# Recurrence and expert layer on one core: when the third group's token rows leave, and the places of slot products, a maximum, a unit's turn and weight pieces

## The chip, the cores and the metric

The kernel runs on one core of a Trainium2 chip. Its metric is the device time in microseconds of one execution. The time before the change is 388.15 us, the median of 6 runs that lie between 387.39 and 389.12 us. A core has a matrix engine (TensorE, called PE in the profile, with PEld for the loading of its weights), VectorE (DVE), ScalarE (ACT), GpSimd (POOL) and SyncE (SP), which issues most of the DMA transfers. Each engine works through its own instructions in order; engines wait for each other by semaphores.

## What is computed

A tanh recurrence over 1024 steps for two sequences, and on its states a layer of eight experts of which each token uses two; the result is added to the input.

```python
xW = jnp.einsum('ntd,dh->nth', x, Wx) + b
def step(prev_h, xw_t):
    next_h = jnp.tanh(xw_t + prev_h @ Wh)
    return (next_h, next_h)
_, hs = jax.lax.scan(step, h0, jnp.swapaxes(xW, 0, 1))
...
logits = x_flat @ gate_w.T
top_v, top_i = jax.lax.top_k(logits, K)
probs = jax.nn.softmax(top_v.astype(jnp.float32), axis=-1).astype(logits.dtype)
combine = jnp.einsum('tk,tke->et', probs, one_hot)
def body(acc, ws):
    wge, wue, wde, we = ws
    hidden = jax.nn.silu(x_flat @ wge.T) * (x_flat @ wue.T)
    return (acc + we[:, None] * (hidden @ wde.T), None)
...
x = x + _L0_ffn_ref(_L0_cond_ref(x, cond_1024, Wx, Wh, b), gate_w, wg, wu, wd)
```

There are 2048 tokens of 256 numbers, 8 experts (E), 1024 hidden numbers per expert (I) and K = 2.

## The kernel before

**The recurrence.** The 1024 steps are cut into 64 chunks of 16 steps per sequence, and all chunks run side by side; each starts early, from a state that isn't exact, and a check at the end compares the starts of the chunks with the ends of the chunks before (`chunk_starts` at L538, `starts_check` at L673). The loop over `s` from 8 to 63 (L612) is one chain: four products of the state with `Wh` (two halves `j` of the output, two halves `k` of the state; eight PE records in float32, L619), two tanh on ScalarE, and `seed` (L307), which puts the input part of step `s + 2` into the accumulators: half 0 on VectorE, half 1 on ScalarE. The last 16 steps, 48 to 63, give the token tiles 0 to 15, each of 128 tokens.

**The route.** While the chain runs, tiles are routed in four groups of four. `route_tile` (L348) is a PE product that turns a tile into rows of 264 numbers, 256 of the state and 8 logits. `route_max` finds the two best experts on VectorE. `route_choice`, `route_position` (PE, L395) and `route_code` give each token its place in the list of its expert; `route_onehot` builds three large one-hot arrays of 128 x 1024 (parts 0, 1 and 2) on VectorE, and `route_slots` (L438) multiplies them on PE into the table `inv_ps`, which says for each slot of each expert which token stands there. `rows_out` (L377) sends a group's rows to `rows_d` in memory by SyncE: two transfers of 256 KB for the states and later one of 16 KB for the weights that replace the logits.

**The gathers.** `early_slots` (L471) runs once groups 0 and 1 are in the table: it computes the index `gidx` for the first 256 slots of expert 0, and two indirect DMAs of GpSimd gather these rows from the first half of `rows_d`. `early_turn` (L480) turns them on PE into the layout that the experts need, and unit 0 starts. `all_slots` (L483) does the same for the rest once group 3 is in: `gidx`, a copy `inv`, two more gathers (the late tiles, for unit 1), and what the order of the experts needs.

**The experts.** A unit is up to 512 slots of one expert. Unit 0 and unit 1 are the two halves of expert 0, unit 2 is expert 1, and the other six experts follow in the order of their counts, worked out by `expert_order` (L492), a generator of five pieces of work that are called one at a time. A unit has eight steps of 128 hidden numbers. One step has a `front` (12 PE products, L717), a `gate` (silu on ScalarE, product on VectorE, then a split of the result into a high half by a ScalarE cast and a low half by VectorE), and a `back` (L879) two steps later. `units[i].turn()` turns the gathered rows of a unit on PE and splits them on ScalarE and VectorE. The next expert's weights are split into high and low halves in six pieces (`Job.piece`, L762: ScalarE 128 x 1024 for the high half, VectorE for the low half); `split_at` says in which step each stands, and an odd piece, once done, issues the load for the expert after it on SyncE.

**The order.** Most instructions stand in the order in which Python issues them (`vec`, `act`, `pool` and `pe(...)` fix it). Around the chain and the first steps of the experts, the order is written as due times: `at(t, f)` files a piece of work and `run(t)` issues all that is due, by time. In step `s` of the recurrence, `run(s - 0.5)` stands after the second of the four products and `run(s)` at the end. In step `n` of the experts, `run` is called with 64 + n + 0.15 after the front, + 0.2 ahead of `shut(n)` (the gate), + 0.3 after it, and + 0.6 after the backs. These calls fix the order on every engine:

```python
if i == 2:
    run(s - 0.5)
...
u.front(s)
run(64 + n + 0.15)
...
run(64 + n + 0.2)
if n > 0:
    shut(n)
```

Unit 0's steps are n = 0 to 7, unit 1's 8 to 15, and unit 2 starts at n = 16. At n = 3 the back of step 0 is issued, at n = 4 those of steps 1 and 2, and from n = 5 on that of step n - 2.

Of the kernel before, what the change touches and what calls it, by code (L numbers as in the profile page):

```python
# [8 lines left out]
F32 = mybir.dt.float32  # L9
# [10 lines left out]
P = 128  # L20
# [4 lines left out]
E = 8  # L25
# [32 lines left out]
def rnn_moe(ctx, tc, xT, xrows, h0T, Wx, Wh, b, gw, W, out):  # L58
    nc = tc.nc
    pe = tc.keep_in_program_order  # L60
# [3 lines left out]
    dram = ctx.enter_context(tc.tile_pool(name="dram", bufs=1, space=DRAM))  # L64
    ov = ctx.enter_context(tc.tile_pool(name="ov", bufs=1))
    wctx = ctx.enter_context(ExitStack())

    rows_d = dram.tile([NT, ROW], F32, name="rows_d")


    ig = cst.tile([P, 2, P + E], F32, name="ig")
# [71 lines left out]
    def ptr_tile():  # L143
        return pl.ptp.tile([P, 512], F32, name="ptr", tag="ptr")
# [53 lines left out]
    def token_parts(pool, n):  # L198
        return [pool.tile([P, 2, n * P], F32R, name=f"{nm}{n}") for nm in ("xhi", "xlo")]
# [120 lines left out]
    early_tiles, late_tiles = [], []  # L320
# [19 lines left out]
    for g in range(R // GRP):  # L340
        o = (g % 2) * 4 * GRP * P
        gr = {"r0": g * GRP, "n": GRP}
# [34 lines left out]
    def rows_out(gr, cs):  # L377
        a, b = gr["r0"] * P, (gr["r0"] + gr["n"]) * P
        for o, e in cs:
            nc.sync.dma_start(rows_d[a:b, o:e].rearrange("(i p) c -> p i c", p=P), gr["rows"][:, :, o:e])  # L380

    def route_exp(gr):
        gr["ex"] = rt.tile([P, gr["n"]], F32, name="ex")
# [73 lines left out]
    def gather(idx, rows=rows_d):  # L457
        xg = pl.gp.tile([P, ROW], F32, name="xg")
        nc.gpsimd.indirect_dma_start(  # L459
            out=xg, out_offset=None, in_=rows[:, :],  # L460
            in_offset=bass.IndirectOffsetOnAxis(ap=idx, axis=0),
        )
        return xg
# [7 lines left out]
    def early_slots():  # L471
# [3 lines left out]
        scatter_index(sidx[:, 0:ET], inv_e, eq_e)  # L475
        early_tiles.extend(gather(gidx[:, i : i + 1], rows_d[0 : NA * P, :]) for i in range(ET))

    x4 = token_parts(pl.xp, MT)

    def early_turn():  # L480
# [63 lines left out]
    def at(step, f, *args):  # L544
        todo.setdefault(step, []).append(lambda: f(*args))

    def run(step):
        for t in sorted(t for t in todo if t <= step):
            for f in todo.pop(t):
                f()  # L550
# [8 lines left out]


    maxima = {r: r + 49.5 for r in range(R)}
    maxima.update({9: 59.5, 10: 60.6, 11: 61, 12: 62.2, 13: 62.3, 14: 64.05, 15: 64.06})
    for g, gr in enumerate(groups):
        for r in range(gr["r0"], gr["r0"] + gr["n"]):
            at(r + 49, route_tile, gr, r)
# [2 lines left out]
    def group(g, choice, exp, position, code, hot, slots):  # L568
        gr = groups[g]
        at(choice, route_choice, gr)  # L570
        at(exp, route_exp, gr)
        at(choice + 0.1, rows_out, gr, ((0, P), (P + E, ROW)))
        at(position, route_position, gr)
        at(code, route_code, gr)
        at(code, rows_out, gr, ((P, P + E),))
        for part, t in enumerate(hot):
            at(t, route_onehot, gr, part)
        for i in range(gr["n"]):
            at(slots, route_slots, gr, i)

    group(0, 52.5, 52.6, 53.5, 53.5, (54, 54, 55), 56.5)
    group(1, 56.5, 56.6, 57.5, 57.5, (58, 58, 58), 59.9)
    at(58.1, early_gap)
    at(60, early_slots)
    group(2, 61, 61.1, 62, 62, (62.4, 64.1, 64.1), 65.12)
    at(63.5, early_turn)
    group(3, 64.07, 64.08, 65.1, 65.13, (65.2, 65.3, 66.3), 67.65)
    at(64.09, act.activation, warm, zl[:, 0:1], AF.Silu)
    at(67.65, all_slots)
    at(68.6, chunk_starts)  # L590

    inj = {}
    for s, q in ((15, 2), (31, 1), (47, 0)):
# [18 lines left out]
    for s in range(S0, 64):  # L612
# [7 lines left out]
        n, late = (s - S0 + 3) // 2, None  # L620
# [35 lines left out]
        n = (s - S0 + 6) // 2  # L656
# [9 lines left out]
    def starts_flag(ps):  # L666

        pe(nc.tensor.matmul(ps, lhsT=ones16, rhs=okh, start=True, stop=True))
        vec.tensor_scalar(flags[:, 0:1], ps, P - 0.5, None, ALU.is_lt)
        vec.tensor_tensor(flags[:, 2:3], flags[:, 0:1], flags[:, 1:2], ALU.add)  # L670
        vec.tensor_copy(flags_i, flags)

    def starts_check():  # L673
        vec.tensor_tensor(df, df, df, ALU.mult)
        vec.tensor_scalar(df, df, TOL * TOL, None, ALU.is_le)
        vec.tensor_reduce(okm, df, AX.XYZ, ALU.min)
        vec.tensor_copy(okh, okm)
# [30 lines left out]
    with ExitStack() as c2:  # L708
# [187 lines left out]
        units = [Unit(jobs[0], cols=ET * P, tiles=early_tiles), Unit(jobs[0], t0=ET, cols=(MT - ET) * P, tiles=late_tiles)]  # L896
# [17 lines left out]
        split_at = {}  # L914
        for j in range(len(jobs) - 1):
            two = sum(u.job is jobs[j] for u in units) > 1
            for n, m in enumerate((2, 3, 4, 6, 7) if not two else (5, 7, 10, 11, 12, 15) if j == 0 else (3, 4, 7, 10, 12, 15)):
                split_at[j, m] = j + 1, n
            if not two:
                split_at[j + 1, 0] = j + 1, 5  # L920
        order_ops = expert_order()

        def shut(n):

            u, s, j, m = step_of(n)
            low = []
            if (j, m) in split_at:
                to, p = split_at.pop((j, m))
                u.gate(s, lambda: low.append(jobs[to].piece(p, jobs[to + 1] if to + 1 < len(jobs) else None)))
            else:  # L930
                u.gate(s)
            for f in low:
                f()
# [8 lines left out]
        for n in range(len(steps)):  # L942
            i, s = steps[n]
            u = units[i]
            u.front(s)

            run(64 + n + 0.15)
            if n == 1:
                shut(0)
# [3 lines that stand above are left out]
            run(64 + n + 0.3)  # L953
            if n == 16:
                starts_check()
            elif n == 20:
                next(order_ops, None)
                starts_flag(ptr_tile()[:, 0:1])

            if s == (6 if i == 0 else 5) and i + 1 < len(units):  # L960
                if i == 0:
                    units[1].gather()
                    units[2].gather()
                units[i + 1].turn()
            for _ in range({4: 1, 6: 1, 8: 2, 9: 1}.get(n, 0)):
                next(order_ops)
            if i > 0 and s == 2 and i + 2 < len(units):
                units[i + 2].gather()
            if n < len(steps) - NIC + TAIL + 2:

                for late in {2: (), 3: (0,), 4: (1, 2)}.get(n, (n - 2,) if n > 4 else ()):
                    v, t = steps[late]
                    units[v].back(t)
            run(64 + n + 0.6)
        assert not split_at

# [181 lines left out]
```

## Time and profile before

| what | value |
|---|---|
| median of 6 runs | 388.15 us (387.39 to 389.12) |
| time of the profiled execution | 387.87 us |
| its span, first to last instruction | 385.9 us |
| mean granted TensorE clock | 0.994 |
| PE waits at route_slots (L442) | 1.7 us in 2 waits |
| PE waits for the early gathers (L208) | 1.6 us in 2 waits |
| early gathers, POOL start | 71.30 and 72.79 us |
| first front of unit 0 | 78.84 us |
| late gathers, POOL start | 90.81 and 92.10 us |
| first front of unit 1, of unit 2 | 98.34, 116.26 us |
| row stores of a 256 KB kind, median to landing | 2.7 us (groups 0, 1, 3), 4.0 us (group 2) |
| gathers through `gidx`, median to landing | 2.9 us |

Times in the timeline count from the start of the span. A line of it gives the start, the duration, the engine, the source line, the operation with what it writes and reads, and in brackets how long the engine had been idle before it and who released it. L54 is the line of a helper through which all instructions of VectorE, ScalarE and some of GpSimd are issued, so there one goes by the names of the tiles: `wd<-iota,m` is a one-hot array (built in the space of a weight tile), `xg<-rows_d,gidx` a gather, `pgu_t<-hl` a seed, `g<-g,pgu_t` the product of a gate. PE's instructions overlap, so the next one starts before the one before is shown to end.

### The profile page before, as it was taken

Reading aid. Unit: us, or ns where it says so; the run is one execution under the profiler, and the core shown is the slowest. Engines: PE = TensorE matmul, PEld = TensorE weight load, DVE = VectorE, ACT = ScalarE, POOL = GpSimd, SP = SyncE. Lnnn points to the kernel's source line nnn. Section 1 sums busy time; section 2 is a strip of 40 time slices with the busy share of each in tenths; the row PEclk is TensorE's granted clock in tenths of the full one; section 3 lists DMA queues with packets and bytes.
Section 4 is the critical chain, followed back from the end, with each engine's and each line's share of the span. In section 5 each row is a group of like instructions: output and inputs, shape, how many; then the busy total and the mean of one; then the engine's idle time right before and its main releaser. Section 6 shows DMA issues by size and latency. Waiting matters only on the chain.

```text
span 385.9 us, 7242 instructions
## 1 busy us (share of the span) xinstructions
PE 369.5 (96%) x2715; PEld 349.4 (91%) x2715; DVE 227.0 (59%) x568; ACT 199.0 (52%) x460; POOL 116.9 (30%) x124
## 2 busy tenths in 40 slices
PE   8999999898999999999999999999999999999990
PEld 8998899788998889999999999999989999999890
DVE  6876648767776566565547554566545645663410
ACT  3746667544565544655446544665354555444420
POOL 3780000304282510783223601522050014006042
PEclk9999999999999999999999999999999999999997
DMA  7962334321465333665145243345133244003122
GB/s 222 404 259 100 109 111 114 87 56 45 140 177 182 60 113 129 151 206 132 48 122 139 57 124 116 59 137 138 44 94 115 59 160 54 0 2 40 12 23 35
DMA packets 19225, 42.20 MB, mean 109 GB/s; under 512 B 4800, under 2 KB 14176, under 8 KB 16064
## 3 DMA queue, kind: packets, MB, share of 16 engines
q1 hardware_dynamic: 12400, 32.32, 24.7%
q0 software_dynamic: 6496, 9.09, 14.6%
q8 instruction: 23, 0.38, 0.4%
q10 hardware_dynamic: 288, 0.26, 0.3%
q14 instruction: 18, 0.15, 0.1%
HBM read 35.15 MB, written 9.14 MB: 115 GB/s over the span
## 4 chain that ended last, share of the span: by engine, by line
PE 86%; DVE 3%; POOL 3%; issue 2%; DMA 2%; ACT 2%; POOLq 0%
PE pgu_t L717 47%; PE yb L879 22%; PE pgu_t L619 9%; PE ptr L301 2%; DMA xg<-rows_d,gidx 2%; PE ptr L208 2%; POOL out_dram L466 2%; DVE wd L54 1%; PE ptr L630 1%; PE ptr L355 1%; ACT h L54 1%; PE pgu_t L879 1%; PE ptr L879 1%; POOL xg L459 1%; DVE hh L54 0%
## 5 line engine op out<-in xcount | busy, mean ns | idle before, releaser
L879 PE MATMUL yb<-wd,hh 128*128 128x256 f32 (+2 forms) x544 | 94.1, 283 | 0.0
L54 DVE TENSOR_TENSOR g<-g,pgu_t 128x256 f32<-128x256 f32 (+5 forms) x96 | 50.1, 522 | 60.0 <-PE pgu_t L717 47.4
L879 PEld LDWEIGHTS yb<-wd,hh 128*128 128x128 f32 (+2 forms) x544 | 80.5, 185 | 1.7
L54 ACT CAST hh<-g 128x256 fp32r<-128x256 f32 (+5 forms) x92 | 44.6, 485 | 69.5 <-DVE g L54 68.7
L466 POOL DMA_INDIRECT out_dram<-y,si x27 | 43.8, 1621 | 118.5 <-ACT y L54 113.0
L717 PE MATMUL pgu_t<-xhi,gu_g 128*128 128x256 f32 (+5 forms) x384 | 78.1, 325 | 0.3 <-ACT xhi L54 0.3
L717 PE MATMUL pgu_t<-xhi,gu_u 128*128 128x256 f32 (+5 forms) x384 | 77.8, 324 | 0.0
L54 ACT ACTIVATE g<-pgu_t 128x256 f32<-128x256 f32 (+5 forms) x96 | 44.8, 467 | 63.8 <-PE pgu_t L717 63.1
L717 PEld LDWEIGHTS pgu_t<-xhi,gu_u 128*128 128x128 f32 x384 | 61.3, 188 | 4.3
L717 PEld LDWEIGHTS pgu_t<-xhi,gu_g 128*128 128x128 f32 x384 | 58.8, 189 | 2.8 <-issue 0.5
L54 DVE TENSOR_TENSOR hl<-g,hh 128x480 fp32r<-128x480 f32 (+4 forms) x52 | 31.0, 597 | 31.8 <-ACT hh L54 31.8
L879 PE MATMUL yb<-wd,hl 128*128 128x256 f32 (+1 forms) x176 | 49.6, 282 | 0.0
L717 PE MATMUL pgu_t<-xlo,gu_g 128*128 128x256 f32 (+5 forms) x192 | 46.6, 324 | 0.0
L717 PE MATMUL pgu_t<-xlo,gu_u 128*128 128x256 f32 (+5 forms) x192 | 46.5, 323 | 0.0
L459 POOL DMA_INDIRECT xg<-rows_d,gi x27 | 29.4, 1090 | 48.9 <-DVE cm L808 19.7
L717 PEld LDWEIGHTS pgu_t<-xlo,gu_g 128*128 128x128 f32 x192 | 32.5, 188 | 2.3
L717 PEld LDWEIGHTS pgu_t<-xlo,gu_u 128*128 128x128 f32 x192 | 32.5, 188 | 2.2
L879 PEld LDWEIGHTS yb<-wd,hl 128*128 128x128 f32 (+1 forms) x176 | 32.2, 183 | 0.1
L54 DVE TENSOR_TENSOR hh<-g,hh 128x256 fp32r<-128x256 f32 x40 | 17.0, 425 | 22.4 <-ACT hh L54 22.4
L619 PE MATMUL pgu_t<-h,wh 128*128 128x128 f32 (+1 forms) x224 | 28.6, 266 | 1.5
L54 ACT ACTIVATE h<-pgu_t 128x128 f32<-128x128 f32 (+1 forms) x72 | 17.6, 276 | 13.8 <-PE pgu_t L619 11.5
L619 PEld LDWEIGHTS pgu_t<-h,wh 128*128 128x128 f32 x152 | 18.4, 190 | 4.3 <-ACT h L54 3.4
(166 smaller groups left out, 462.4 us busy)
## 6 DMA issues: line engine op xcount, KB each, us to landing
raw<-in_W_dram SPq DMA_DIRECT2D x24, 1024.0 KB, 5.0
gu_u<-in_xT_dram SPq DMA_DIRECT2D x6, 256.0 KB, 4.8
rows_d<-gu_u SPq DMA_DIRECT2D x6, 256.0 KB, 2.7
out_dram<-in_xrows_dram SPq DMA_DIRECT2D x1, 512.0 KB, 15.0
rows_d<-rows SPq DMA_DIRECT2D x2, 256.0 KB, 4.0
xg<-rows_d,gi POOLq DMA_INDIRECT x27, 3.2
out_dram<-y,si POOLq DMA_INDIRECT x27, 3.9
gu_u<-in_xT_dram ACTq DMA_DIRECT2D x2, 128.0 KB, 3.6
```

What stands on the lines that cost most here:

```text
L54: return lambda *a, **k: self.tc.keep_in_program_order(f(*a, **k))
L208: pe(nc.tensor.transpose(pt[:, m, j, :], tiles[i][:, k * (P + E) : k * (P + E) + P], ident))
L301: pe(nc.tensor.matmul(pt, lhsT=l, rhs=r, start=(i == 0), stop=(i == len(ops) - 1)))
L355: pe(nc.tensor.matmul(pt[:, k * P : (k + 1) * P + E], lhsT=hall[k][:, r, :], rhs=ig[:, k, :], start=(k == 0), stop=(k == 1), skip_group_ch ...
L459: nc.gpsimd.indirect_dma_start(out=xg, out_offset=None, in_=rows[:, :], in_offset=bass.IndirectOffsetOnAxis(ap=idx, axis=0),)
L466: return nc.gpsimd.indirect_dma_start(out=out[:, :], out_offset=bass.IndirectOffsetOnAxis(ap=idx, axis=0), in_=y, in_offset=None, compute_ ...
L619: pe(nc.tensor.matmul(acc[s % 2][j], lhsT=w[:, k, j * P : (j + 1) * P], rhs=prev[k], start=False, stop=True, skip_group_check=True))
L630: pe(nc.tensor.matmul(pt, lhsT=zl, rhs=zl, start=True, stop=True))
L717: pe(nc.tensor.matmul(pt, lhsT=a[i], rhs=b[j], start=(i + j + n == 0), stop=(j == 1 and n == len(lhs_rhs) - 1), skip_group_check=True))
L879: pe(nc.tensor.matmul(yt[0:w, :], lhsT=h[a][:, i * P : i * P + w], rhs=wd[b][:, ic, :], start=(ic == 0 and first and n == 0), stop=(ic == ...
```

## The change

Group 2's rows are held: a small store to a new tensor `landed` in memory reads the last early gather's tile and stands ahead of them on SyncE's queue, and all row stores keep the program's order. Group 1's slot products and `early_slots` move from the end of step 60 to the middle of step 61 (59.9 and 60 to 60.1 and 60.2). The maximum of tile 5 moves from the middle of step 55 to its end. Group 3's slot products and `all_slots` move from behind the front of n = 4 to behind the backs of n = 4 (67.65 to 68.55). `chunk_starts` moves from n = 4's end to n = 6's. The pieces of expert 1's weights move from n = 5, 7, 10, 11, 12 and 15 to n = 8, 10, 12, 14, 15 and 16. `units[1].gather()` and `units[2].gather()` move from n = 6 to n = 5 (unit 1's rows are already on their way then), unit 1's turn from ahead of the back at n = 6 to behind it, unit 3's gather from n = 10 to n = 11. The five pieces of `expert_order` move from n = 4, 6, 8, 8, 9 to n = 6, 7, 9, 9, 11.

```diff
+    landed = dram.tile([1, E], F32, name="landed")
...
     def rows_out(gr, cs):
         a, b = gr["r0"] * P, (gr["r0"] + gr["n"]) * P
         for o, e in cs:
-            nc.sync.dma_start(rows_d[a:b, o:e].rearrange("(i p) c -> p i c", p=P), gr["rows"][:, :, o:e])
+            pe(nc.sync.dma_start(rows_d[a:b, o:e].rearrange("(i p) c -> p i c", p=P), gr["rows"][:, :, o:e]))
...
         early_tiles.extend(gather(gidx[:, i : i + 1], rows_d[0 : NA * P, :]) for i in range(ET))
+
+        pe(nc.sync.dma_start(landed, early_tiles[-1][0:1, 0:E]))
...
-    maxima.update({9: 59.5, 10: 60.6, 11: 61, 12: 62.2, 13: 62.3, 14: 64.05, 15: 64.06})
+    maxima.update({5: 55, 9: 59.5, 10: 60.6, 11: 61, 12: 62.2, 13: 62.3, 14: 64.05, 15: 64.06})
...
-    group(1, 56.5, 56.6, 57.5, 57.5, (58, 58, 58), 59.9)
+    group(1, 56.5, 56.6, 57.5, 57.5, (58, 58, 58), 60.1)
     at(58.1, early_gap)
-    at(60, early_slots)
+    at(60.2, early_slots)
     group(2, 61, 61.1, 62, 62, (62.4, 64.1, 64.1), 65.12)
     at(63.5, early_turn)
-    group(3, 64.07, 64.08, 65.1, 65.13, (65.2, 65.3, 66.3), 67.65)
+    group(3, 64.07, 64.08, 65.1, 65.13, (65.2, 65.3, 66.3), 68.55)
     at(64.09, act.activation, warm, zl[:, 0:1], AF.Silu)
-    at(67.65, all_slots)
-    at(68.6, chunk_starts)
+    at(68.55, all_slots)
+    at(70.6, chunk_starts)
...
-            for n, m in enumerate((2, 3, 4, 6, 7) if not two else (5, 7, 10, 11, 12, 15) if j == 0 else (3, 4, 7, 10, 12, 15)):
+            for n, m in enumerate((2, 3, 4, 6, 7) if not two else (8, 10, 12, 14, 15) if j == 0 else (3, 4, 7, 10, 12, 15)):
                 split_at[j, m] = j + 1, n
-            if not two:
+            if j == 0 or not two:
                 split_at[j + 1, 0] = j + 1, 5
...
-            if s == (6 if i == 0 else 5) and i + 1 < len(units):
-                if i == 0:
-                    units[1].gather()
-                    units[2].gather()
+            if n == 5:
+                units[1].gather()
+                units[2].gather()
+            if i > 0 and s == 5 and i + 1 < len(units):
                 units[i + 1].turn()
-            for _ in range({4: 1, 6: 1, 8: 2, 9: 1}.get(n, 0)):
+            for _ in range({6: 1, 7: 1, 9: 2, 11: 1}.get(n, 0)):
                 next(order_ops)
-            if i > 0 and s == 2 and i + 2 < len(units):
+            if i > 0 and s == (3 if i == 1 else 2) and i + 2 < len(units):
                 units[i + 2].gather()
             if n < len(steps) - NIC + TAIL + 2:
 
                 for late in {2: (), 3: (0,), 4: (1, 2)}.get(n, (n - 2,) if n > 4 else ()):
                     v, t = steps[late]
                     units[v].back(t)
+            if n == 6:
+                units[1].turn()
             run(64 + n + 0.6)
```

## The prediction

> **What bounds the kernel now.** I read the page first. TensorE (PE) is busy for 369.5 of 385.9 us and holds 86% of the chain that ended last, so only what makes PE wait can be won. Next I asked for PE's own waits over the whole span: the three largest after the start-up are the ones this change touches. Then I followed each in the timeline, together with VectorE (DVE), GpSimd (POOL) and SyncE's queue (SPq).
>
> ```profile
> PE 369.5 (96%) x2715; PEld 349.4 (91%) x2715; DVE 227.0 (59%) x568; ACT 199.0 (52%) x460; POOL 116.9 (30%) x124
> ```
>
> ```profile
> PE yb L442 <- DVE wd L54: 1.7, 2, 1.3
> PE pgu_t L208 <- DMA xg<-rows_d,gidx: 1.6, 2, 0.8
> ...
> PE pgu_t L717 <- ACT xhi L54: 0.3, 1, 0.3
> ```
>
> The first line is the page's busy time, the others are PE's waits; columns of the waits: total us, times, longest. L442 is route_slots, L208 the turn of gathered rows, L717 a front, L879 a back. The timeline of the first two waits:
>
> ```profile
> 70.01 0.62 PE L442 MATMUL yb<-wd 128*128 128x128 f16 x8 [0.40 <-DVE wd L54]
> ...
> 70.13 0.28 DVE L54 COPY pgu_t<-hl 128x128 f32<-128x128 f32 x1
> ...
> 70.86 0.15 DVE L54 TENSOR_SCALAR gidx<-yb 128x2 int32<-128x2 f32 x1
> ...
> 71.30 1.19 POOL L459 DMA_INDIRECT xg<-rows_d,gidx  x1 [3.35 <-DVE eq_e L54]
> ...
> 71.59 4.30 SPq L380 DMA_DIRECT2D rows_d<-rows  x3
> ...
> 72.79 0.97 POOL L459 DMA_INDIRECT xg<-rows_d,gidx  x1 [0.30 <-issue]
> ...
> 76.43 0.30 PE L208 MATMUL pgu_t<-ident,xg 128*128 128x128 f32 x1 [0.78 <-DMA xg<-rows_d,gidx]
> 77.53 0.31 PEld L208 LDWEIGHTS pgu_t<-ident,xg 128*128 128x128 f32 x3 [0.98 <-DMA xg<-rows_d,gidx]
> ```
>
> The two early gathers start at 71.30 and 72.79 and PE takes them up at 76.43 and 77.53: 5.13 and 4.74 us, though the eight gathers of this form have a median of 2.9 to landing. Group 2's rows were issued between them, at 71.59, and in this stretch both DMA queues move packets at once. The third wait, and what follows it:
>
> ```profile
> 88.54 0.68 DVE L54 TENSOR_TENSOR wd<-iota,m 128x1024 f16<-128x1024 f16 x1
> ...
> 89.28 0.62 PE L442 MATMUL yb<-wd 128*128 128x128 f16 x8 [1.28 <-DVE wd L54]
> ...
> 89.71 1.68 PE L879 MATMUL pgu_t<-wd,hh 128*128 128x256 f32 x12
> ...
> 90.37 0.17 DVE L54 TENSOR_SCALAR gidx<-yb 128x18 int32<-128x18 f32 x1
> ...
> 90.81 0.98 POOL L459 DMA_INDIRECT xg<-rows_d,gidx  x1 [6.96 <-DVE inv L54]
> ...
> 91.23 0.64 PE L717 MATMUL pgu_t<-xhi,gu_g 128*128 128x256 f32 x4
> ...
> 92.10 1.19 POOL L459 DMA_INDIRECT xg<-rows_d,gidx  x1 [0.30 <-issue]
> ...
> 94.78 0.88 PE L208 MATMUL ptr<-ident,xg 128*128 128x128 f32 x4
> ```
>
> Here the reader should see that the late pair is just in time: the chain of waits gives its second gather 2.98 us, to 95.08, and PE stands at its transposes from 94.78. From 98.34 on the fronts follow each other every 2.13 us (98.34, 100.47, 102.60) without a wait. All the play is therefore between 69 and 97 us.
>
> **Part 1, group 1's slots and the early gathers.** The slots move from after step 60 to the middle of step 61. PE leaves step 60 at 69.45 (68.56 + 0.89, the issue time of a step's eight records as between 70.99 and 71.88), and now does the route tile first (to 69.91). Step 61's first two blocks need the seed that DVE writes at 70.13 to 70.41, behind the same one-hots, so they start at about 70.47 and take 0.45; the slots follow at 70.92 (0.43), the other blocks end at 71.80. Before, that was 71.88: a gain of 0.08, which I take as 0. But the last slot product now ends at 70.92 + 0.62 = 71.54 instead of 70.63, so gidx is computed at 71.59, not 70.86: 0.73 later. Queued on DVE behind it are step 63's seed, two maxima and group 2's choice; they slip by 0.3, which may hold the position products of 73.70 by 0.14. That lies before a wait for the gather and costs nothing. Maximum 5 moves behind the seed of step 57 (63.16 on DVE, becomes 62.81); PE's gain of 0.2 there ends at group 0's slots at 64.10, which wait for the same one-hot. Taken as 0.
>
> POOL starts 0.44 after gidx (70.86 to 71.30, 90.37 to 90.81): 72.03. The second starts 1.29 later, as in the late pair: 73.32. With the rows held back, nothing else is on the DMA engines, as with the late pair; I take the median of 2.9: landing at 76.22 instead of 77.53, **-1.31**. The bounds use the group's own extremes, 2.7 with the shortest spacing (1.25) and the 3.1 median of all gathers with the early pair's spacing (1.49): 75.98 and 76.62, so -1.55 to -0.91. PE is ready at 75.03 + 0.46 + 0.14 = 75.63, earlier than all of these.
>
> A page argues for much less. The Trainium skill, "DMA: Bandwidth & Descriptors", Queues, rings and completion order, says that each DMA engine takes turns between the queues packet by packet; a gather could then lose only about its own transfer time to the rows: 135 KB at the 287 GB/s that the rows reached alone is 0.47. By that, landing would stay at 4.27, the gain here would vanish (77.59) and the whole change would end 0.46 slower. The late pair's 2.98 in an empty queue is the nearer measurement, and I go by it.
>
> **The new wait on SP.** SP's landed store waits for the second gather, and behind it in order are three row stores of group 2 and three of group 3, seven issues of 0.36, or 2.5 us. Group 2's rows then leave at about 76.6; group 3's, issued at 79.01 before, can land behind them by about 85 (2.7 to 5.2 each by this profile). Their only reader left is the late gathers at 90.8 or later, so nothing is paid; SP's next job is a weight load at 102.23. Without that cover of some 5 us the late pair would slip one for one.
>
> **Part 2, group 3's slots.** PE has issued front 4 by 86.42 + 1.42 = 87.84 and stands until 89.28. Now the backs of steps 1 and 2 fill this (1.42, to 89.26; step 2's low half ends on DVE at 88.62, before it is needed). The one-hot of 88.54 ends at 89.22, so the slots run at 89.28 and front 5 starts at 89.71 instead of 91.23: 1.52 earlier. Back 3 (0.71), front 6 (1.42) and back 4 (0.71) bring PE to the turn, now behind back 4, at 89.71 + 1.42 + 0.71 + 1.42 + 0.71 = 93.97.
>
> Where does the stall go? all_slots now stands on DVE behind the gate of step 4. After step 3's low half (90.03) its four links follow as in step 3: product at 90.37, ScalarE's cast 0.45 later, DVE's low half 0.44 later at 91.26, gidx 0.34 later at 91.60. That is 1.23 after the old 90.37. POOL starts at 92.04 and 93.33, landing is at 96.23, and PE waits 2.2 us. From the second tile to the next front takes 0.38 (77.53 to 77.91): front 7 starts at 96.61, before at 96.21: **+0.40**. With the same bounds, 2.7 and 1.25, 3.1 and 1.49, it is +0.16 to +0.80. So the 1.28 of the removed wait isn't won; it is paid at the turn. The two splits of the turned rows still hide under front 7 and back 5 (2.13 against some 1.7 from 96.57 to 98.3).
>
> **Part 3, what only moves.** Six weight pieces (ScalarE 1.05, DVE 1.22 each), five steps of expert_order, chunk_starts (0.48) and the gathers of units 2 and 3 change place; none is removed. PE has no wait in that stretch, so there is nothing to win. The tight place is piece 3, now at step 14: with step 14's gate and the turn of unit 2 (two DVE splits, 1.29) ahead of it, its low half ends near 118.6, and front 16 needs it at about 116.7 + 1.4 + 0.7 = 118.8. I take 0, up to +1.2 (one low half). Piece 5 meets starts_check at step 16: 0.68 + 0.69 + 1.22 + 1.28 = 3.9 of DVE in a step of 3.52 of PE, caught up in step 17. The first load of the next job slips from 102 to about 109; its first piece is cut near 126 and a load lands in 5.0.
>
> **The sum.** -1.31 + 0.40 = -0.91. The profiled execution took 387.87 (span 385.9 and 1.97 around it): 386.96. The median of the runs, 388.15, stands 0.28 above that execution; from it, 387.24, so 387.2. Own range of this case: -1.39 to -0.11 from the bounds, 386.8 to 388.0.
>
> **Rivals.**
> The rows are not what slowed the early gathers (or they aren't held). Then the pair starts 0.53 later than now (73.32 against 72.79) and lands as late as before, 4.74: 78.06, +0.53, and with the turn +0.93: **389.1**, slower. For it: the first gather of a stretch, with few packets beside it at first, took 5.13. Against: group 2's rows themselves had a median of 4.0 against 2.7 for the other groups, so each slowed the other. It decides from a landing time of 3.8 on (2.9 + 0.91).
>
> The late pair comes in time, if DVE reaches gidx well before 91.60. Then front 7 starts at 93.97 + 0.40 = 94.37, -1.84, and with -1.31 **385.0**. For it: all 1.28 of the wait would be won. Against: DVE runs in a fixed order, and its links from 88.54 leave no gap.
>
> The late pair is slower than taken, since four gathers of unit 2 follow closely and PE stands there in full view: at 3.6 instead of 2.9 (the 27 later gathers have a median of 3.2, the longest of all took 6.1) the sum is -0.2, **387.9**, no change.
>
> Piece 3 is late at front 16 by a whole low half: -0.91 + 1.2 = +0.3, **388.4**.
>
> **How the numbers follow.** This kernel can tell about 0.2%, 0.78 us, from no change. The forecast gets 0.62, of which 0.42 lies beyond -0.78 and 0.20 within; slow gathers in any case 0.12 (slower); late pair in time 0.10 (faster); late pair slower 0.09 (same); piece 3 late 0.07 (0.04 same, 0.03 slower). Faster 0.52, same 0.33, slower 0.15. The range of 386.0 to 388.9 leaves out most of the full win and most of the slow-gather case.
>
> **What would show it.** Right: group 2's rows on SPq after 76, the second early gather taken up 2.9 after its start, front 0 some 1.3 earlier; no wait at group 3's slots, but one of about 2 us at the turn of unit 1, and then fronts every 2.13 us up to unit 2. Wrong: early gathers still at 4.7, a turn without a wait or with 3 us, or PE waiting at front 16 for weights.

## The result and the profile after

The changed kernel takes 388.61 us in the median of 39 runs (387.13 to 390.49), the kernel before, run beside it, 387.70 us (81 runs, 386.81 to 390.35). The ratio is 1.0018 with a 95% interval of 1.0009 to 1.0026: slower by some 0.7 us, where 387.2 us and faster had been forecast. The profiled execution of the changed kernel took 389.37 us, with a span of 387.3 us and a mean granted clock of 0.989 (before: 387.87, 385.9 and 0.994).

First the page of the changed kernel: busy time, and the granted clock in 40 slices of the span.

```profile
PE 371.3 (96%) x2715; PEld 351.3 (91%) x2715; DVE 227.3 (59%) x568; ACT 199.2 (51%) x460; POOL 117.8 (30%) x124
...
PEclk9999999999899999999999999999999999999997
```

PE has the same 2715 instructions as before and is busy 1.8 us longer. Waits do not do that: e2_starts, below, has the same waits at the turn and is busy for 369.2 us. The slice with an 8, the eleventh, begins at about 97 us (10 x 9.7). Next PE's own waits in the changed kernel (total us, times, longest):

```profile
PE ptr L210 <- DMA xg<-rows_d,gidx: 1.9, 2, 1.2
...
PE pgu_t L210 <- DMA xg<-rows_d,gidx: 0.5, 1, 0.5
PE pgu_t L623 <- ACT rows L54: 0.5, 1, 0.5
...
PE yb L883 <- ACT y L54: 0.2, 1, 0.2
PE yb L444 <- DVE wd L54: 0.2, 1, 0.2
```

L210 is now the line of a turn (208 before), L444 route_slots (442), L721 a front (717), L883 a back (879). The wait at route_slots has gone (1.7 to 0.2), the early turn waits less (1.6 to 0.5), and a new wait of 1.9 us stands at unit 1's turn (`ptr`). Two small ones are new as well: 0.5 of the chain (L623) for a copy of `rows` on ScalarE, in step 61, and 0.2 of a back for `y`. So far this is what was forecast. The timeline of the early gathers after the change:

```profile
73.38 0.99 POOL L461 DMA_INDIRECT xg<-rows_d,gidx  x1 [0.30 <-issue]
...
76.28 0.55 PE L210 MATMUL pgu_t<-ident,xg 128*128 128x128 f32 x3 [0.49 <-DMA xg<-rows_d,gidx]
...
76.66 1.51 SPq L382 DMA_DIRECT2D rows_d<-rows  x3
...
77.60 0.59 PE L721 MATMUL pgu_t<-xhi,gu_g 128*128 128x256 f32 x3 [0.30 <-ACT xhi L54]
```

Group 2's rows leave at 76.66, and the second early gather is taken up 2.90 us after its start, 4.74 before. Front 0 starts at 77.60 instead of 78.84. Then the late gathers:

```profile
88.05 0.62 PE L444 MATMUL yb<-wd 128*128 128x128 f16 x8
...
90.36 0.17 DVE L54 TENSOR_SCALAR gidx<-yb 128x18 int32<-128x18 f32 x1
...
93.70 0.33 PE L210 MATMUL ptr<-ident,xg 128*128 128x128 f32 x1 [0.73 <-DMA xg<-rows_d,gidx]
...
95.21 0.61 PE L210 MATMUL ptr<-ident,xg 128*128 128x128 f32 x3 [1.18 <-DMA xg<-rows_d,gidx]
...
95.52 1.18 PE L721 MATMUL pgu_t<-xhi,gu_g 128*128 128x256 f32 x4
...
99.25 0.64 PE L721 MATMUL pgu_t<-xhi,gu_g 128*128 128x256 f32 x4
```

The slots run without a wait, the index is ready late (POOL starts the gathers at 90.81 and 92.09), and PE stands at the turn. Look at the last two lines: four products of one form take 1.18 us at 95.52 and 0.64 at 99.25. From front 7 (95.52) to front 8 (99.25) pass 3.73 us, where the kernel before needs 2.13, and PE has no wait in between. The windows of the changed kernel (busy time and instructions of PE, PEld, DVE, ACT and POOL, then the granted clock, the DMA share and GB/s) name the reason:

```profile
94.00:96.00 2.00, 0.82 (x6) 0.79 (x6) 0.66 (x4) 0.14 (x1) 1.48 (x2) 0.89 0.50 131
96.00:98.00 2.00, 2.00 (x12) 2.00 (x11) 1.09 (x3) 0.45 (x1) 1.60 (x2) 0.50 0.39 101
98.00:100.00 2.00, 2.00 (x15) 2.00 (x15) 0.62 (x2) 0.79 (x2) 0.39 (x1) 0.76 0.37 106
```

Behind the pause the granted clock is 0.50 for all of 96 to 98 us. What is missing from 1.00 adds up to 2 x (0.11 + 0.50 + 0.24) = 1.70 us; at half speed that is 3.4 us of time. It also gives the mean clock: 1.70 / 387 = 0.004, from 0.994 to about 0.989.

Last, the timeline of the changed kernel some 30 us later, where unit 2 begins:

```profile
125.27 0.69 DVE L54 TENSOR_TENSOR g<-g,pgu_t 128x512 f32<-128x512 f32 x1
...
125.99 0.62 ACT L54 CAST hh<-g 128x512 fp32r<-128x512 f32 x1 [3.04 <-DVE g L54]
...
126.52 0.83 ACT L54 ACTIVATE y<-yb,xg 128x256 f32<-128x256 f32 x2
...
127.41 0.50 PE L883 MATMUL yb<-wd,hh 128*128 128x256 f32 x2 [0.23 <-ACT y L54]
```

VectorE is held up by a weight piece and by `starts_check`, so its gate product comes at 125.27; ScalarE, in order, stands 3.04 us for it, and behind that cast is the scaling of unit 1's output, which reads the accumulator `yb` that the back of step 16 must have. Front 18 to front 19 takes 4.72 us (124.21 to 128.93), 4.24 before.

**The bill.** By the starts of the fronts: front 0 is 1.24 earlier, front 7 still 0.69, front 8 is 0.91 later (+1.60), front 16 the same 0.91 (117.17 against 116.26), front 19 +1.39 (+0.48), and the spans differ by 1.4. So these steps hold 1.39 of the 1.4.

**Two kinds of executions.** The record holds 41 executions of the changed kernel in this comparison, the profiled one among them. They fall apart by span and clock: 22 have 385.3 to 386.7 us at 0.990 to 0.994, and 19 have 387.1 to 388.4, all at 0.989 or 0.990. The profiled one is of the second kind. The mean clock alone does not part them (three of the first kind have 0.990 too), since it is low anyway at the end of the span, where PE has finished: 0.50 from 384 us on in the profiled execution.

### The profile page after: what moved, and what is told of

Same layout as the page of the kernel before. It is cut to its first block, busy times and chain, and to the rows that moved or that the text cites. A ratio compares the mean times of both kernels' runs of the same rounds, so it can differ in the third digit from the quotient of the medians.

```text
span 387.3 us, 7243 instructions
## 1 busy us (share of the span) xinstructions
PE 371.3 (96%) x2715; PEld 351.3 (91%) x2715; DVE 227.3 (59%) x568; ACT 199.2 (51%) x460; POOL 117.8 (30%) x124
## 4 chain that ended last, share of the span: by engine, by line
PE 81%; DVE 7%; ACT 4%; POOL 2%; DMA 2%; issue 1%; POOLq 0%; DVEq 0%; ACTq 0%
PE pgu_t L721 42%; PE yb L883 21%; PE pgu_t L623 9%; PE ptr L303 3%; PE ptr L210 2%; POOL out_dram L468 2%; DMA xg<-rows_d,gidx 2%; ACT hh L54 2%; DVE wd L54 1%; DVE g L54 1%; DVE hh L54 1%; PE pgu_t L278 1%; PE ptr L634 1%; PE ptr L357 1%; PE ptr L288 1%
## 5 line engine op out<-in xcount | busy, mean ns | idle before, releaser
L883 PE MATMUL yb<-wd,hh 128*128 128x256 f32 (+2 forms) x544 | 94.2, 283 | 0.2 <-ACT y L54 0.2
L883 PEld LDWEIGHTS yb<-wd,hh 128*128 128x128 f32 (+2 forms) x544 | 80.5, 185 | 2.3 <-ACT y L54 0.7
L721 PE MATMUL pgu_t<-xhi,gu_g 128*128 128x256 f32 (+5 forms) x384 | 78.7, 327 | 0.3 <-ACT xhi L54 0.3
L721 PE MATMUL pgu_t<-xhi,gu_u 128*128 128x256 f32 (+5 forms) x384 | 78.2, 325 | 0.0
L721 PEld LDWEIGHTS pgu_t<-xhi,gu_u 128*128 128x128 f32 x384 | 61.8, 189 | 4.3
L721 PEld LDWEIGHTS pgu_t<-xhi,gu_g 128*128 128x128 f32 x384 | 59.1, 190 | 2.8 <-issue 0.5
L883 PE MATMUL yb<-wd,hl 128*128 128x256 f32 (+1 forms) x176 | 49.6, 282 | 0.0
L721 PE MATMUL pgu_t<-xlo,gu_g 128*128 128x256 f32 (+5 forms) x192 | 46.8, 325 | 0.0
L721 PE MATMUL pgu_t<-xlo,gu_u 128*128 128x256 f32 (+5 forms) x192 | 46.7, 325 | 0.0
L461 POOL DMA_INDIRECT xg<-rows_d,gi x27 | 30.7, 1135 | 50.5 <-DVE cm L812 19.7
L721 PEld LDWEIGHTS pgu_t<-xlo,gu_g 128*128 128x128 f32 x192 | 32.7, 189 | 2.3
L721 PEld LDWEIGHTS pgu_t<-xlo,gu_u 128*128 128x128 f32 x192 | 32.7, 189 | 2.2
L883 PEld LDWEIGHTS yb<-wd,hl 128*128 128x128 f32 (+1 forms) x176 | 32.2, 183 | 0.1
L623 PE MATMUL pgu_t<-h,wh 128*128 128x128 f32 (+1 forms) x224 | 28.6, 266 | 1.5
L623 PEld LDWEIGHTS pgu_t<-h,wh 128*128 128x128 f32 x152 | 18.4, 190 | 4.3 <-ACT h L54 3.4
```

The costliest lines, as they stand in the source:

```text
L461: nc.gpsimd.indirect_dma_start(out=xg, out_offset=None, in_=rows[:, :], in_offset=bass.IndirectOffsetOnAxis(ap=idx, axis=0),)
L623: pe(nc.tensor.matmul(acc[s % 2][j], lhsT=w[:, k, j * P : (j + 1) * P], rhs=prev[k], start=False, stop=True, skip_group_check=True))
L721: pe(nc.tensor.matmul(pt, lhsT=a[i], rhs=b[j], start=(i + j + n == 0), stop=(j == 1 and n == len(lhs_rhs) - 1), skip_group_check=True))
L883: pe(nc.tensor.matmul(yt[0:w, :], lhsT=h[a][:, i * P : i * P + w], rhs=wd[b][:, ic, :], start=(ic == 0 and first and n == 0), stop=(ic == ...
```

## The experiments

The theory: what was won at the gathers is paid back by a lowered clock behind the pause at the turn, and by the order of step 16. The rivals: the pause alone is dear, whatever the clock; or the two kinds differ by something else. Ratios are to the kernel before on the same chip: 387.69 us (35 runs) in the first group, 389.75 (29) in the second, 390.31 (29) in the third.

### First group: four parts one by one

**e1_fill** puts eight products of zeros into the pause.

```diff
             if n == 6:
+                fill = ptr_tile()[:, 0:P]
+                for _ in range(8):
+                    pe(nc.tensor.matmul(fill, lhsT=zl, rhs=zl, start=True, stop=True, skip_group_check=True))
                 units[1].turn()
```

> The changed kernel, with eight products of zeros (into a spare bank that nobody reads) on PE ahead of unit 1's turn; they take about 1.8 us of the 2.4 us in which PE otherwise stands there. Theory A (the pause at the turn lowers the granted clock for some us, and this costs about 1.6 us in about half of the executions): no execution with a mean clock of 0.989 or 0.990 is left, all are at 0.993 to 0.994; front 7 starts where it did (about 95.5 us) and lasts 1.42 us, not 2.67; spans near 385.7, none above 386.8; the median falls by 0.5 to 1.0 us against the changed kernel's 388.61. Rival B (the drop of the clock has nothing to do with that pause): the two kinds of executions stay, about half with a span above 387.

Measured: 387.81 us, ratio 0.9997 (0.9985 to 1.0010). Front 7 to front 8 takes 2.20 us (96.29 to 98.49) and the clock from 95 to 100 us is 1.00. All 12 spans lie between 385.5 and 386.6; the long kind is absent. Not all clocks are at 0.993 or above, as had been expected: two of these short executions have 0.990. Front 7 stands at 96.29 because this execution is 0.88 later from group 0's slots on (64.68 against 63.80). The term of step 16 is still paid (front 18 to 19 takes 4.68, 0.44 more than before).

**e2_starts** moves the check of the starts one step on, away from piece 5.

```diff
-            if n == 16:
+            if n == 17:
```

> The changed kernel, with starts_check one step later (17 instead of 16), so that it does not meet the sixth weight piece on VectorE. Theory A: the pause at the turn is untouched, so about half of the executions keep a clock of 0.989 and a span near 387; in either kind the wait at the first back of unit 2 (0.23 us by the waits, 0.45 between issues) is gone, so all spans are 0.3 to 0.5 us shorter. Rival C (the backlog on VectorE and ScalarE at step 16 is what makes the change slow): the whole loss of 0.7 to 0.9 us goes, the median is that of before or less.

Measured: 387.70 us, ratio 1.0008 (0.9994 to 1.0022). Front 18 to 19 is back at 4.24 us (122.45 to 126.69), the value before: it was the check of the starts beside piece 5 that cost the 0.48. This profiled execution happens to be one with no drop, and it has the pause all the same. Its timeline of PE:

```profile
93.52 0.33 PE L210 MATMUL ptr<-ident,xg 128*128 128x128 f32 x1 [0.71 <-DMA xg<-rows_d,gidx]
94.99 0.55 PE L210 MATMUL ptr<-ident,xg 128*128 128x128 f32 x3 [1.14 <-DMA xg<-rows_d,gidx]
95.29 0.72 PE L721 MATMUL pgu_t<-xhi,gu_g 128*128 128x256 f32 x4
...
97.50 0.64 PE L721 MATMUL pgu_t<-xhi,gu_g 128*128 128x256 f32 x4
```

The same two waits (0.71 and 1.14), and front 8 follows front 7 after 2.21 us. The pause by itself therefore costs only its length; the drop, where it comes, costs 3.73 - 2.21 = 1.52 more. Of the 12 executions three were long (386.5 to 387.3 us at 0.986 or 0.990), fewer than the half that had been expected. The median is that of before, as rival C had it, so the median doesn't settle between the two; the long executions that remain show that the backlog of step 16 isn't the whole loss.

**e3_order** puts the gate of step 4 behind the slot products and `all_slots`, so that the index no longer waits for the gate.

```diff
-            if n > 0:
+            if n > 0 and n != 4:
                 shut(n)
...
             run(64 + n + 0.6)
+            if n == 4:
+                shut(4)
```

> The changed kernel, with the gate of step 4 issued behind group 3's slots and all_slots instead of ahead of them. Theory A: gidx is computed 1.2 us earlier (near 89.2 instead of 90.36), the late pair starts near 89.6 and 90.9 and lands near 94, PE waits about 1.0 us at the turn instead of 1.9, front 7 starts near 94.3 instead of 95.5; the clock stays at 0.993 or better in nearly all executions, so the median falls by 1.2 to 2 us, to 386.5 to 387.3, faster than before. If the wait at the turn is set by something other than gidx (the gathers themselves), front 7 stays near 95.5.

Measured: 386.95 us, ratio 0.9979 (0.9963 to 0.9994). Spans of 384.2 to 385.9, none long. Its timeline of PE shows one wait at the turn where there were two:

```profile
94.28 0.55 PE L210 MATMUL ptr<-ident,xg 128*128 128x128 f32 x3 [0.87 <-DMA xg<-rows_d,gidx]
94.58 0.72 PE L721 MATMUL pgu_t<-xhi,gu_g 128*128 128x256 f32 x4
...
96.80 0.64 PE L721 MATMUL pgu_t<-xhi,gu_g 128*128 128x256 f32 x4
```

The gathers start 0.9 us sooner (89.91 and 91.20), though this execution is 0.33 later at front 0, and front 7 follows front 0 after 16.65 us instead of 17.92: 1.27 won, with no instruction removed, and no drop behind it.

**e4_rows** takes of the whole change only the held rows: the kernel before with the store to `landed` and with the row stores in program order.

```diff
-            nc.sync.dma_start(rows_d[a:b, o:e]...)
+            pe(nc.sync.dma_start(rows_d[a:b, o:e]...))
...
+        pe(nc.sync.dma_start(landed, early_tiles[-1][0:1, 0:E]))
```

> The kernel before with one part of the change alone: group 2's rows held until the second early gather has landed; all else stands as before. Theory (the early gathers were slowed by these rows): gathers start at 71.3 and 72.8 as before and the second is taken up at 75.6 to 75.9 instead of 77.5, so front 0 starts 1.6 to 1.9 us earlier, at 77.0 to 77.2, and as the rest moves with it, the span is shorter by as much: 384.0 to 384.3, a ratio of 0.995 to 0.996. Rival (something after the gathers gives it back, as in the changed kernel): front 0 as said, but less than 0.8 us of it left at the end.

Measured: 386.30 us, ratio 0.9966 (0.9955 to 0.9977). The timeline of the early turn in it:

```profile
75.39 0.78 PE L209 MATMUL pgu_t<-ident,xg 128*128 128x128 f32 x4
...
76.93 0.71 PE L719 MATMUL pgu_t<-xhi,gu_g 128*128 128x256 f32 x4 [0.30 <-ACT xhi L54]
```

All four transposes run without a wait (group 2's rows leave at 76.00, behind them), front 0 is 1.91 earlier than before and the span 1.8 shorter (384.1). By the ratio the gain is 1.3 us, a little less than had been expected. This one part is worth more alone than within the change, and it keeps the wait of 1.3 us at group 3's slots; with this single wait none of its 12 executions is below 0.990. At the early gathers PE has nothing left to wait for.

### Second group: the clock again, the move to step 61, and the best order

**e5_same** is the changed kernel itself, with no edit, beside **e5_fill**, which is e1_fill once more.

> The changed kernel itself, beside the next three on one chip. Theory A: its executions are of two kinds, 0.3 us or so below those of before where the clock stays whole, and 1.3 to 1.7 us longer than that where the pause at unit 1's turn (2.4 us between PE's issues) makes the clock drop; between 2 and 8 of the 12 are of the second kind (span near 387 or above).

> The changed kernel with eight products of zeros ahead of unit 1's turn, a second time, now beside the changed kernel on the same chip. Theory A: hardly an execution with a span of 387 or above (at most 1 of 12), median 0.3 to 0.9 us below the changed kernel's on this chip. Rival B (the pause isn't what brings the long executions): as many long ones as the changed kernel has.

Measured: e5_same 389.27 us, 0.9985 (0.9963 to 1.0007), with six spans of 386.3 to 386.8 at 0.992 to 0.994 and six of 387.6 to 388.9 at 0.988 or 0.989. So the two kinds are a trait of the kernel and come up again on another chip. By its interval the changed kernel is not shown to be slower on this chip, where the kernel before is itself spread from 385.8 to 390.2 us, seven of its 29 executions below 0.990. e5_fill has no execution below 0.990, as expected; but its median, 389.47 us, 0.9989 (0.9968 to 1.0011), did not fall. Its profiled execution pays elsewhere: ScalarE starts the gate of step 7 at 99.61 instead of 97.95, the stretches from front 16 to 17 and from front 18 to 19 take 3.80 and 5.28 us, and the span is 388.0. The expectations on the median and on the spans were missed: nine of the 12 spans are at 387.2 us or above, where one at most had been expected. Only the low clock is gone.

**e6_step60** puts group 1's slots and `early_slots` back to step 60.

```diff
-    group(1, 56.5, 56.6, 57.5, 57.5, (58, 58, 58), 60.1)
+    group(1, 56.5, 56.6, 57.5, 57.5, (58, 58, 58), 59.9)
...
-    at(60.2, early_slots)
+    at(60, early_slots)
```

> The changed kernel with group 1's slots and early_slots back at the end of step 60 (59.9 and 60). If moving them to the middle of step 61 only delays the early gathers: the gathers start 0.7 us earlier (71.3 and 72.8), front 0 starts 0.6 us earlier than in the changed kernel, all that follows moves with it, the pause at the turn stays; spans 0.6 us shorter than the changed kernel's, kind by kind. If the move pays elsewhere (the recurrence's steps 61 to 63), less than 0.2 us.

Measured: 387.81 us, ratio 0.9946 (0.9927 to 0.9965). Front 0 starts 12.93 us after group 0's slots, against 13.80 in the changed kernel and 14.74 before: between these two profiles the move to step 61 cost 0.87 us. The other profiles give a wider range: with the rows held, front 0 comes 12.87 to 13.37 after group 0's slots where the slots stand at step 60 (e4_rows, e6_step60, e7_all, f0_pause, f1_fill, f3_all), and 13.70 to 13.81 where they stand in step 61, so the move costs 0.3 to 0.9. Three of 12 executions are long, at 0.989. Kind by kind, by medians, the spans are 1.2 and 1.7 us below those of e5_same, more than the 0.6 expected; what makes up the rest isn't shown.

**e7_all** joins three edits: step 60 for group 1's slots, the gate of step 4 behind `all_slots`, and the check of the starts in step 17.

> The changed kernel with three things undone or moved: slots of group 1 and early_slots at the end of step 60, the gate of step 4 behind all_slots, starts_check at step 17. The terms add: -0.6 for the first, -0.9 to -1.2 for the second (pause at the turn 1.1 us instead of 2.4, too short for the clock to drop), -0.45 for the third: against before -2.3 to -2.8 in executions with a whole clock, a median near 385.2, ratio 0.993 to 0.995.

Measured: 385.93 us (6 runs, 385.31 to 387.06), ratio 0.9896 (0.9867 to 0.9926); spans of 383.3 to 384.9. It beats both kernels, and by more than the terms had given (0.993 to 0.995).

### Third group: is it the drop, with the other costs gone?

**f0_pause** is the changed kernel with step 60 and the check in step 17; the pause stays. **f1_fill** is the same with the eight products of e1_fill. Read as a pair, they part the drop from the rest.

> The changed kernel with group 1's slots back at step 60 and starts_check at step 17, so that only the pause at unit 1's turn is left of what slowed it; the base for the next run. Theory A: two kinds of executions, spans near 384.6 with a whole clock and 1.3 to 1.7 us more, with a mean clock of 0.989 or 0.990, in a quarter to a half of them. If the long kind came from starts_check or the moved slots, it is gone.

> The kernel of the run before this one, and eight products of zeros ahead of unit 1's turn. Theory A: the long kind is gone (at most 1 of 12 executions with a clock at or below 0.990 and a span over 1.2 us above the shortest), the shortest spans are as those of the run before. Rival B (the pause has nothing to do with it): as many long ones as there.

Measured: f0_pause 388.14 us, 0.9946 (0.9921 to 0.9972): seven executions of 384.5 to 386.4 us at 0.993 or 0.994 and five of 386.9 to 387.3 at 0.989 or 0.990. So the long kind comes neither from the check nor from the moved slots. f1_fill 388.25 us, 0.9946 (0.9926 to 0.9967): spans from 385.9 to 387.4, no cluster at a low clock. The ratio is the same: filling the pause removes the long kind and brings no gain here. For its shortest span is 1.4 us above f0_pause's shortest, which was not expected. One line of ScalarE from each timeline, f0_pause first, shows where it begins:

```profile
97.07 0.38 ACT L54 ACTIVATE g<-pgu_t 128x256 f32<-128x256 f32 x1 [0.88 <-PE pgu_t L721]
```

```profile
99.07 0.39 ACT L54 ACTIVATE g<-pgu_t 128x256 f32<-128x256 f32 x1 [3.02 <-PE pgu_t L721]
```

Both are the gate of step 7. In f1_fill front 7 starts earlier (95.06 against 95.32) and the clock is 1.00, and yet ScalarE takes its result up 2.0 us later. What follows is then late in turn: front 8 to 16 takes 18.50 us instead of 17.91, front 16 to 17 3.97 instead of 3.52, with a wait for piece 3's low half. Why ScalarE comes late with the products of zeros isn't settled; in the profile of e1_fill, on the first chip, it isn't late (98.04, 1.75 us after front 7).

**f2_before** asks whether the kernel before has drops too: six products of zeros ahead of its early turn and six ahead of group 3's slots.

```diff
+    def zeros(n):
+        fill = ptr_tile()[:, 0:P]
+        for _ in range(n):
+            pe(nc.tensor.matmul(fill, lhsT=zl, rhs=zl, start=True, stop=True, skip_group_check=True))
...
+        zeros(6)
...
+    at(67.64, zeros, 6)
```

> The kernel before with six products of zeros ahead of the early turn and six ahead of group 3's slots, where PE pauses 1.9 and 1.4 us between its issues. If the longer executions of before (7 of 35 on one chip with a span above 386.7 and a clock of 0.991 or less) come from the clock dropping at these pauses, they are gone, and the shortest spans stay as before's (385.3 to 385.8 there); the median falls by 0 to 0.4 us. If not, they stay.

Measured: 389.71 us, ratio 0.9977 (0.9956 to 0.9998). The kernel before had six of 29 executions at 0.986 or 0.987, spans of 389.1 to 391.4 us; with the products none of 13 is below 0.990. Six of 29 against none of 13 is a hint, not a proof. One of the 13 has a span of 390.9 us; there the clock is 0.66 from 10 to 15 us, at the start of the work, and front 8 to 16 and front 18 to 19 take 18.72 and 5.53 us instead of 17.92 and 4.24.

**f3_all** repeats e7_all.

> The kernel of e7_all again, for its interval on another chip: the changed kernel with group 1's slots at step 60, the gate of step 4 behind all_slots and starts_check at step 17. By the terms found so far, -1.87 for the rows, and -0.3 to -0.7 for the rest (PE waits 0.9 at the turn instead of 1.3 at group 3's slots, and unit 2 starts 1.7 us earlier than before): a ratio of 0.993 to 0.995, no execution with a clock of 0.989.

Measured: 386.88 us (6 runs), ratio 0.9903 (0.9870 to 0.9936), spans of 383.3 to 385.2 and no clock below 0.990. The gain is again larger than the 0.993 to 0.995 expected. In its profile the terms add up to 2.6 us between group 0's slots and front 19 (60.82 against 63.44); the ratio says 3.8. The kernel before is spread over 386.5 to 391.4 us on this chip, and what makes up the difference isn't shown. Its page, busy time and granted clock:

```profile
PE 369.1 (96%) x2715; PEld 349.6 (91%) x2715; DVE 227.5 (59%) x568; ACT 198.7 (52%) x460; POOL 118.3 (31%) x124
...
PEclk9999999999999999999999999999999999999997
```

PE is busy 2.2 us less than in the changed kernel with the same 2715 instructions, and no slice has an 8. At the turn of unit 1 PE has one wait of 0.7 us, as in e3_order. Front 7 starts 16.53 us after front 0, and front 18 to 19 takes 4.24.

## Why the prediction was wrong

**The early gathers: right, with one size off.** The held rows brought the landing to 2.90 us, as taken. The start was forecast 0.53 later; counted from group 0's slots the second gather now starts at 9.58 us instead of 8.69, 0.89 later. Of the 0.36 between the two, 0.15 lies ahead of the index (it is computed 7.64 after group 0's slots, where 6.76 + 0.73 = 7.49 was forecast; ahead of the slots PE now waits 0.48 for the rows' copy in step 61), and 0.20 in the spacing of the two gathers: it is 1.49 as it was before, and the late pair's 1.29 had been taken. Counted so, front 0 gained 14.74 - 13.80 = 0.94, not 1.31; the other 0.30 of the 1.24 in the trace is an earlier start of this execution, and group 0's slots stand between 63.6 and 64.8 in the profiles of the changed kernel and its variants. e4_rows and e6_step60 show the two parts: holding the rows is worth 1.8 in the trace, and the move to step 61 takes 0.87 of it back (0.3 to 0.9 over all profiles). The small delay of some 0.47 that the prediction weighed and set aside was rightly set aside: holding the rows took 4.74 - 2.90 = 1.84 off.

**SP's queue and the late rows: right.** Group 3's rows were stored from 78.27 on, in 4.74 us, well before the late gathers at 90.81.

**Group 3's slots and the stall that moves: right.** The wait has gone from route_slots, and the index came at 90.36, which is the forecast 91.60 less the 1.24 that the whole stage is earlier. The second late gather landed after 3.12 us instead of 2.9. Front 7 is +0.55 by front 0, where +0.40 was taken: a size within its bounds.

**The step that failed: the price of PE's pause.** The prediction had "POOL starts at 92.04 and 93.33, landing is at 96.23, and PE waits 2.2 us", and of the wait removed it said "it is paid at the turn". The length was right (the trace has 0.73 and 1.18, with one transpose between), and only the length was priced; the opening claim, that only what makes PE wait can be won, left out that PE's own work can take longer. Of the signs that the prediction named for being right, the one that failed is this: front 8 follows front 7 after 3.73 us, not 2.13. The runs show a second price of the pause, due in 19 of 41 executions: the granted clock falls to 0.50 for about 3.4 us, and front 7 with back 5 takes 3.73 us instead of 2.21. Of 48 executions of e2_starts, e5_same, e6_step60 and f0_pause, which keep the pause, 17 are of the long kind, 11 of them at 0.989 or less; of the 60 in which it is filled (e1_fill, e5_fill, f1_fill) or cut to one wait (e3_order, e7_all, f3_all), none is below 0.990, and their spans show no second group (those of e5_fill are long throughout, 386.5 to 388.3 us). That the pause brings the drop on is shown by this; that each long execution without a profile had its drop at this very place is inferred from its mean clock, which fits 1.70 us at 387.

**The second step that failed: "caught up in step 17".** The prediction set VectorE's 3.9 us against a step of PE, took the backlog at nothing, and did not follow what it held up meanwhile: the scaling of unit 1's output, queued on ScalarE behind the late cast, reads an accumulator that the back of step 16 needs. It cost 0.48, and without the check in step 16 it is gone (e2_starts).

**Piece 3: right.** No wait at front 16 in the changed kernel; only f1_fill shows that the cover is thin.

**The sum.** The forecast was -0.91. From group 0's slots on, the profiles give -0.94 for the early gathers (forecast -1.31), +0.55 up to front 7 (forecast +0.40), +0.08 for front 7 itself (2.21 after the turn, 2.13 before) and +0.48 in step 16: +0.17 without a drop. A drop adds 1.52, which makes +1.69, as the profiled execution has it (1.39 at front 19, and 0.30 for its earlier start). With 19 drops in 41 the mean is 0.17 + 0.70 = +0.87 us, to be set against the measured ratio, 0.7 us (0.35 to 1.0). By its clocks the kernel before may have drops of its own: 18 of its 93 executions on the three chips of the experiments are below 0.990. That would make the two differ by somewhat less. The forecast was also counted from the median of six runs, and 81 runs put that 0.45 lower. So even without any drop the change as a whole would have been worth nothing: its best part was eaten by the move to step 61, the later late gathers and the order in step 16.

## What to carry to other kernels

Where a change gathers PE's waits into one place, price the pause at its length and, beside that, a slowed stretch behind it. Here two short waits with a single small instruction between them brought the drop on; a single wait of 1.30 us (e4_rows) or 0.87 us (e3_order) did not in 12 executions each. When busy time grows at the same count of instructions, look at the granted clock in short windows before looking for a wait. When pieces of work move along an engine with a fixed order, follow each thing queued behind them on the other engines to the buffer that it frees, and not just the one that the engine itself fills.

## What the runs showed of the hardware

In the profiled execution the drop follows a pause of 2.24 us (92.97 to 95.21, with 0.33 of one transpose in it), and 19 of 41 executions of the same program are of its kind. The Trainium skill, "TensorE: Matmul & The Clock Gate", HAM oscillation, gives the rule that PE should have no idle gap above about 3.4 us. The measurement decides against it as a safe bound: no single gap here is above 1.2 us. The half clock (0.50) and the 3.4 us worked out for its length agree with that page's Part 1, which tells of a window of 3.4 us that runs freely; that the phase of such a window decides between the two kinds would fit, but no run here shows it.

Two stores of 256 KB beside two gathers had stretched these: the median to landing of the two early gathers was 4.8 us, and it is 2.9 as soon as the stores are held.

With products of zeros in the pause no execution on any of three chips was below 0.990, but on two of them something else took its place; avoiding the pause (e3_order, e7_all) was the better way. The late start of ScalarE that came with the filling, 1.7 and 2.0 us, stays open.
